# A new order for the opening of a gated-delta attention block: VectorE's first scans, the gates and the first seven keys, and the first unit's work under the substitution

## Chip, core and metric

The kernel runs on one core of one Trainium2 chip. The metric is the device time of one execution in microseconds (us), the median of the runs; less is better. The engines are called PE (TensorE, matmuls and transposes), PEld (its weight loads), DVE (VectorE), ACT (ScalarE), POOL (GpSimd) and SP (SyncE, which issues DMAs). ACT issues DMAs too, and these stand in ACT's own queue.

## What is computed

All inputs are float32. `x` and `fside` are (4, 512, 512), batch by tokens by channels. The reference, cut to what matters:

```python
x = x + attn(wkv(x, fside, fside, w, u, cond), W_qkvz, W_ba, conv_w, dt_bias, A_log, norm_w, W_out)
x = x + ffn(wkv(x, fside, fside, w2, u2, cond), weight, bias)     # signs of weight times its row mean

def wkv(r, k, v, w, u, cond):                 # k = v = fside; decay per channel from w and cond
    ek = exp(min(k, 30)); ekv = ek * v
    nf, df = scan(a = a*decay + ekv_t), scan(b = b*decay + ek_t)         # forward in time
    nb, db = the same scans backward
    euk = exp(min(u + k, 30))
    num = nf + nb - ekv + euk*v;  den = df + db - ek + euk
    return sigmoid(r) * num / max(den, 1e-8) * (0.8 + 0.2*tf)            # tf from cond

def attn(x, ...):                             # 16 query/key heads, 32 value heads of 128
    q, k, v, z = projections of x; a, b = x @ W_ba
    q, k, v = silu(causal convolution of 4 taps along tokens)
    beta = sigmoid(b); g = -exp(A_log) * softplus(a + dt_bias)
    q, k = rmsnorm of both; delta rule in chunks:
        M = strictly lower part of (beta k) k^T * decay(g);  T = (I + M)^-1
        state, out = recurrence over the chunks with T, k, v, q and decay(g)
    return (norm_w * rmsnorm(out) * silu(z)) @ W_out
```

## The kernel before

A **unit** `n` is one batch with one query/key head and its two value heads: 4 x 16 = 64 units. Each unit has six weight slabs of 128 rows: r = 0 query, 1 key, 2 and 3 values, 4 and 5 z. Tokens are taken in four chunks of 128; a chunk's two heads give eight 128x128 matrices M per unit. In batch 0 a slab is loaded (`slab_start`), transposed on PE (`slab_turn`) and copied by ACT (`slab_end`), which also stores it for the later batches.

**The loop** runs over `i`; iteration `i` works on several units at once by a written plan of 22 slots (`plan`, L1044): the recurrence of unit `i-1` (`chunk_w`, `chunk_t`, `chunk_r`), the output of `i-2` and `i-3`, values, query and inverse of unit `i` and the key of unit `i+6`. The order of the plan is the order of every engine's queue. Four units make a group: the 32x32 diagonal blocks of their M go to memory (`key_blocks`), come back with one block to a partition (`group_load`), are inverted by 30 steps of substitution (`group_step`, `group_end`), stored (`blocks_n`, `blocks_t`) and loaded for each unit (`inverse_load`: four `inv_t` and six `inv_n` loads); `inverse_1` to `inverse_4` join them into T. In the loop GpSimd does the substitution; the first group's is done by VectorE.

**The opening** is what has to be there before the loop can run: the first wkv for batch 0 in four channel blocks `cb` (`first_turn` ... `first_end`), written as stages that overlap from block to block; the weights of the gates; the gates (`gates_product` ... `gates_rows`), whose sums go to memory and come back to all partitions (`gap_load`, 512 KB each); keys of units 0 to 5 (projection, taps, Silu, norm by Newton steps, `key_factors`, `key_matrix`); the first group's substitution; and the inverse loads of units 0 and 1. Then the loop begins with `i` = 0, which does unit 0's slabs 2, 3 and 0, values, query and inverse, and unit 6's key. Tiles that later hold other things are lent to the opening (`lent`, `homes`). PSUM has four tags: `pp` 2 banks, `pj` 3, `inv` 1, `st` 2.

A wkv block of the opening, as DVE sees it: limits (`first_limit`), four scans over 512 tokens, `den` from the sum in PSUM, its reciprocal, and the end that writes `cT`. GpSimd makes `ekv` and the terms with `u` (`first_mix`, three products); PE adds the three parts of each sum with the identity (`first_sum`). The order that the stages come in, and where slabs stand among them, is given by this:

```python
for cb in range(KT):
    w = wkv_start(0, 0, cb)
    for i, f in enumerate(stages):
        work.append((i + 4 * cb, cb, f, w))
for i, (_, cb, f, w) in enumerate(sorted(work, key=lambda s: s[:2])):
```

Of the kernel before, what the change touches and what calls it, by code (L numbers as in the profile page):

```python
# [16 lines left out]
P = 128  # L17
# [23 lines left out]
def kernel(  # L41
# [104 lines left out]
    with ExitStack() as main:  # L146
# [24 lines left out]
        for cb in range(KT):  # L171
            at = slice(cb * P, (cb + 1) * P)
            raw = ld.tile([P, NC, P], F32, tag="raw", name=f"raw_k_first_{cb}")
            for t, src in ((raw, fside), (xs[0][:, :, at], x)):
                A.dma_start(out=t, in_=src[0, :, at].rearrange("(c p) d -> p c d", p=P))
            first_raw[cb] = raw

# [4 lines left out]
        for n, v in enumerate((w1, w2, u1, u2)):  # L182
            Q.dma_start(out=wu[:, n, :], in_=v.rearrange("(n p) -> p n", p=P))
        Q.dma_start(out=alog, in_=A_log.partition_broadcast(P))
# [17 lines left out]
        A.activation(nea, alog, AF.Exp)  # L202
        V.tensor_scalar_mul(nea, nea, -1.0)

# [128 lines left out]

        def gates_series(g):

            b, y, e = g["b"], g["y"], g["e"]
            V.tensor_scalar_add(beta[b], beta[b], 1.0)
            V.reciprocal(beta[b], beta[b])
# [21 lines left out]
        def gates_keep(g):  # L360
# [13 lines left out]
                gsum[b][:, 0].rearrange("p c (q r) -> p q c r", r=2),  # L374
            )

        def gates_turn(g):
            g["pt"] = bank("pj", f"ps_gt_{g['b']}")
            T.transpose(g["pt"][: NC * HV, :P], g["flat"][:, : NC * HV], ident)

        def gates_rows(g):
            b, n = g["b"], NC * HV
            rows = wkp.tile([P, S], F32, tag="d", name=f"sp_r_{b}")
            A.copy(rows[:n, :P], g["pt"][:n, :P])
            Q.dma_start(out=gsc[b].rearrange("q (x t) -> (q x) t", t=P), in_=rows[:n, :P])
# [142 lines left out]


# [36 lines left out]
        def key_root(n):  # L566
            root(*units[n]["kroot"])
            key_factors(n)
# [89 lines left out]
        def inverse_load(n):  # L658
# [3 lines left out]
            for d, at in enumerate(blocks):  # L662
# [3 lines left out]
                if d < 3:  # L666
                    for h in range(2):
                        Q.dma_start(
                            out=Tn[blocks[2 * h + (d > 0)], :, at],
                            in_=blocks_n[g, i, d, h * HM : (h + 1) * HM].rearrange("m i j -> i m j"),  # L670
                        )
# [363 lines left out]
        def last_add(b, c):  # L1035
# [80 lines left out]
        INVERSE = (  # L1116
            inverse_1, inverse_1_end, inverse_2, inverse_2_end, inverse_3, inverse_3_end,
            inverse_4, inverse_4_end,
        )

# [27 lines left out]
        for i in range(2):  # L1148
            homes.append(u2p.tile([P, S], F32, tag="q", name=f"lent_q_{i}"))

# [47 lines left out]

        def first_end(w):
            cb, den = w["cb"], w["df"]  # L1200
            e = cT[0][:, cb]
            V.scalar_tensor_tensor(den, w["sum_d"], 1e-8, e, ALU.max, ALU.mult)
            V.reciprocal(den, den)
            V.scalar_tensor_tensor(e, w["sum_n"], scale[:, 0:1], den, ALU.mult, ALU.mult)

        work = []
        stages = (
            first_turn, first_bound, first_limit, first_x, first_mix, (first_scan, "d"), (first_sum, "d"),
            (first_scan, "n"), (first_sum, "n"), first_end,
        )  # L1210
        for cb in range(KT):
            w = wkv_start(0, 0, cb)
            for i, f in enumerate(stages):
                work.append((i + 4 * cb, cb, f, w))
        turned = 0
        for i, (_, cb, f, w) in enumerate(sorted(work, key=lambda s: s[:2])):
            f, *args = f if isinstance(f, tuple) else (f,)
            f(w, *args)
            if i % 6 == 5 and turned < AHEAD:
                if turned == 0:  # L1220
                    for n in range(AHEAD):
                        if n < 2:
                            slab_start(n, 1, homes[n])
                if turned + 2 < AHEAD:
                    slab_start(turned + 2, 1, homes[turned + 2])
                slab_turn(turned, 1)
                slab_end(turned, 1)
                turned += 1
        for n in range(turned, AHEAD):
            slab_turn(n, 1)  # L1230
            slab_end(n, 1)


        wba_raw = ld.tile([2 * HV, D], F32, tag="raw", name="wba_raw")
        Q.dma_start(out=wba_raw, in_=W_ba)
        wbaT = wp.tile([P, KT, 2 * HV], F32, name="wbaT")
        ps = bank("pj", "ps_wba")
        for k in range(KT):
            T.transpose(
                ps[:, k * 2 * HV : (k + 1) * 2 * HV], wba_raw[:, k * P : (k + 1) * P],  # L1240
                ident[: 2 * HV, : 2 * HV],
            )
        A.copy(wbaT.rearrange("p k o -> p (k o)"), ps[:, : KT * 2 * HV])

        cw = wp.tile([P, 4 * HQ, 4], F32, name="cw")
        Q.dma_start(out=cw, in_=conv_w.rearrange("(n p) k -> p n k", p=P))
        g = {"b": 0}

        def first_key(n, tag="pp"):
            project(n, 1, 0, tag)  # L1250
            project(n, 1, 1, tag)

        def first_conv(n):
            tap(n, 1, 0)
            taps(n, 1)

# [213 lines left out]
```

## Time and profile before

| | us |
|---|---|
| median of three runs (lowest, highest) | 3143.19 (3143.12, 3145.72) |
| the profiled execution | 3145.25 |
| its span | 3143.2 |
| PE busy in the span | 2991.7 |
| last `cT` of the first wkv ends | 62.8 |
| DMA issue of the gate sums | 77.3 |
| VectorE's last `key_matrix` of the first group ends | 113.9 |
| first substitution step, end of the transposed copy | 120.6, 143.7 |
| `chunk_w(0,0)`, the start of iteration 1 | 196.3 |
| `chunk_w(1,0)`, the start of iteration 2 | 238.6 |

The times of events are counted from the start of the span. In the lines of a profile, "x" with a number is the count of instructions, and an arrow in brackets names what ended the idle time before an instruction. Most instructions are recorded by one helper, so all have line L80, and tiles tell them apart: `lent_...` are tiles of the first wkv, `dkd` and `dkt` the decay matrices, `L` and `Lt` the blocks of a group, `ps_w` a slab in PSUM or a recurrence product, `wraw` a slab as loaded, `rs_y` and `rs_t` the Newton steps.

### The profile page before, as it was taken

What the parts mean: (1) busy time and instruction counts of PE and PEld (TensorE: products, weight loads), DVE (VectorE), ACT (ScalarE), POOL (GpSimd) and SP (SyncE); (2) the same over time, 40 slices, a digit from 0 to 9 for tenths busy, and PEclk for the clock granted to TensorE, in tenths of its full rate; (3) what the DMA queues carried; (4) which work ended last, traced back from release to release, by engine and by line L of the source; (5) the groups of instructions that cost most, each with busy time, mean ns of one, the idle gap of its engine ahead of it and who ended that gap; (6) DMA issues with size and microseconds to landing.
All of it is one profiled execution on the core that took longest, in us unless ns stands there. A gap on an engine that the chain in (4) does not pass through costs nothing.

```text
span 3143.2 us, 57926 instructions
## 1 busy us (share of the span) xinstructions
PE 2991.7 (95%) x20058; PEld 1979.9 (63%) x20058; DVE 2066.1 (66%) x4738; ACT 1861.3 (59%) x5115; POOL 1313.4 (42%) x3044
## 2 busy tenths in 40 slices
PE   6489999999999999999999999999999999999998
PEld 3256666666666666666666666666666666665664
DVE  7546767667665777668766776667765656577642
ACT  2446666666666666556665666566666666655542
POOL 3216354263522646164432646255442515255302
PEclk9689999999999999999999999999999999999999
DMA  3334544444434323332332422332332322333321
GB/s 75 90 87 140 144 122 127 119 141 132 137 111 142 111 68 92 95 94 85 108 104 89 126 69 88 109 91 84 114 94 74 113 83 84 110 89 96 105 84 54
DMA packets 421875, 320.52 MB, mean 102 GB/s; under 512 B 220176, under 2 KB 329232, under 8 KB 421200
## 3 DMA queue, kind: packets, MB, share of 16 engines
q1 hardware_dynamic: 417360, 314.73, 34.5%
q8 instruction: 160, 2.62, 0.4%
q10 hardware_dynamic: 4224, 2.10, 0.3%
q14 instruction: 131, 1.07, 0.1%
HBM read 246.19 MB, written 70.52 MB: 101 GB/s over the span
## 4 chain that ended last, share of the span: by engine, by line
PE 72%; DVE 17%; ACT 8%; issue 2%; DMA 1%; SPq 0%; POOL 0%; ACTq 0%; DVEq 0%; POOLq 0%
PE ps_p L80 20%; PE ps_out L80 13%; PE ps_z L80 11%; DVE y L80 5%; PE ps_w L80 4%; PE ps_s L80 4%; PE ps_o L80 3%; PE ps_kq L80 2%; PE ps_st L80 2%; DVE f L80 2%; PE ps_f L80 2%; PE ps_j L80 2%; PE ps_i L80 1%; PE ps_v L80 1%; ACT y L80 1%
## 5 line engine op out<-in xcount | busy, mean ns | idle before, releaser
L80 PE MATMUL ps_p<-cT,w 128*128 128x512 f32 x2000 | 956.4, 606 | 13.6 <-ACT w L80 13.6
L80 DVE SCALAR_TENSOR_TENSOR y<-ps_p,cw,y 128x511 f32<-128x511 f32 (+2 forms) x768 | 573.2, 746 | 436.3 <-ACT y L80 421.6
L80 PEld LDWEIGHTS ps_p<-cT,w 128*128 128x128 f32 x2000 | 346.7, 191 | 307.7 <-issue 263.4
L80 PE MATMUL ps_z<-w,cT 128*128 128x256 f32 x2048 | 476.5, 379 | 0.0
L80 PE MATMUL ps_out<-wo,hT 128*128 128x512 f32 x1024 | 465.6, 597 | 7.1 <-DMA wo<-wosc 7.1
L80 PEld LDWEIGHTS ps_z<-w,cT 128*128 128x128 f32 x2048 | 373.7, 190 | 42.5
L80 PEld LDWEIGHTS ps_out<-wo,hT 128*128 128x128 f32 x1024 | 185.5, 191 | 194.8 <-issue 189.4
L80 ACT ACT_TABLE_LOAD x137 | 175.8, 1283 | 160.6 <-DVE y L80 115.9
L80 POOL TENSOR_TENSOR L<-L,t 128x30 f32<-128x30 f32 (+14 forms) x450 | 248.7, 553 | 34.9
L80 ACT ACTIVATE qs<-ps_s,eg 128x128 f32<-128x128 f32 x384 | 120.3, 364 | 239.4 <-PE ps_j L80 136.3
L80 POOL TENSOR_TENSOR t<-L 128x30 f32<-128x30 f32 (+14 forms) x450 | 228.3, 507 | 43.8 <-DMA L<-blocks_m 13.9
L80 POOL TENSOR_SCALAR_AFFINE_SELECT dkd<-dkd 128x1024 f32<-128x1024 f32 x64 | 70.0, 1094 | 396.8 <-DMA dkd<-gsc 272.9
L80 ACT ACTIVATE y<-ps_p,cw 128x512 f32<-128x512 f32 x256 | 173.9, 679 | 70.2 <-PE ps_p L80 69.2
L80 POOL TENSOR_TENSOR rs_t_o<-rs_y_o 128x8 f32<-128x8 f32 x192 | 38.7, 202 | 416.9 <-DVE rs_y_o L80 406.9
L80 ACT ACTIVATE junk<-o 128x128 f32<-128x128 f32 x512 | 157.9, 308 | 75.7 <-DVE o L80 67.6
L80 POOL TENSOR_TENSOR rs_t_k<-rs_y_k 128x4 f32<-128x4 f32 x174 | 55.8, 321 | 348.5 <-DVE rs_y_k L80 339.4
L80 ACT ACTIVATE v<-y 128x512 f32<-128x512 f32 x128 | 80.7, 630 | 203.6 <-DVE y L80 201.0
L80 DVE SCALAR_TENSOR_TENSOR o<-o,rs_y_o,nz 128x128 f32<-128x128 f32 x512 | 189.8, 428 | 1.2 <-POOL rs_y_o L80 1.2
L80 DVE TENSOR_TENSOR x<-x,ps_out 128x512 f32<-128x512 f32 x256 | 168.9, 679 | 25.1 <-PE ps_out L80 24.9
L80 DVE SCALAR_TENSOR_TENSOR r<-ps_s,nbe,vb 128x128 f32<-128x128 f32 x384 | 115.8, 343 | 93.1 <-PE ps_s L80 93.1
L80 ACT COPY w<-ps_w 128x256 f32<-128x256 f32 (+1 forms) x346 | 145.4, 431 | 46.6 <-PE ps_w L80 46.4
L80 ACT ACTIVATE dkt<-dkt,gsum 128x128 f32<-128x128 f32 x512 | 162.6, 392 | 17.4 <-POOL dkt L80 17.3
(270 smaller groups left out, 5565.0 us busy)
## 6 DMA issues: line engine op xcount, KB each, us to landing
w<-wsc SPq DMA_DIRECT2D x288, 256.0 KB, 4.9
dkd<-gsc SPq DMA_DIRECT2D x64, 512.0 KB, 4.3
dkt<-gsc SPq DMA_DIRECT2D x64, 512.0 KB, 4.7
wraw<-in_L_attn_W_qkvz_dram SPq DMA_DIRECT2D x96, 256.0 KB, 3.0
wo<-wosc SPq DMA_DIRECT2D x96, 256.0 KB, 3.7
wsc<-w SPq DMA_DIRECT2D x90, 256.0 KB, 2.1
blocks_m<-dkd SPq DMA_DIRECT2D x256, 32.0 KB, 2.5
L<-blocks_m SPq DMA_DIRECT2D x16, 512.0 KB, 4.9
```

Source lines behind the costliest of these rows:

```text
L80: return lambda *args, **kw: tc.keep_in_program_order(op(*args, **kw))
```

## The change

- Of the eight loads of the first wkv, the two of block 0 stay on ACT's queue; six go to SP, behind three of the small loads. `nea` moves behind the gates' exponentials.
- The first wkv has a written order. `first_end` is split into `first_under`, `first_over` and `first_end`; the limits of the next block stand before the reciprocal, and `first_mix` of the next block is issued beside it. Twelve slabs (keys of units 0 to 6, the gates' weights, unit 0's r = 2, 3, 0) are turned between the sums. Keys of units 0 and 1, and the gates, are summed by channel block as each `cT` comes.
- The logarithm of the gates stands before beta; the cumulative sums are copied from PSUM directly; `gates_turn` uses the gates' bank.
- Keys of the first group: the squares go to GpSimd, the norms to the bank of the gate sums, and Newton steps of two units at a time to VectorE (`root_now`, nine instructions in place of twelve on GpSimd).
- Iteration 0 is gone. Unit 0's work, its z products and the projections of units 4 to 6 stand before the substitution in the queues. `inverse_load` does all `inv_t` loads first; for unit 0 the `inv_n` loads are on ACT's queue. Keys of units 4 to 6 end behind the substitution and in iteration 1 (`job`).

The diff, without names of tiles that only move and without the old order of the opening (shown above). Leading blanks are cut by eight.

```diff
...
-for cb in range(KT):
+def first_load(cb, queue):
     at = slice(cb * P, (cb + 1) * P)
     raw = ld.tile([P, NC, P], F32, tag="raw", name=f"raw_k_first_{cb}")
     for t, src in ((raw, fside), (xs[0][:, :, at], x)):
-        A.dma_start(out=t, in_=src[0, :, at].rearrange("(c p) d -> p c d", p=P))
+        queue.dma_start(out=t, in_=src[0, :, at].rearrange("(c p) d -> p c d", p=P))
     first_raw[cb] = raw
+first_load(0, A)
 tf = const.tile([P, B], F32, name="tf")
 tcond = u2p.tile([P, B, cond.shape[1]], F32, tag="y", name="tcond")
 Q.dma_start(out=tcond, in_=cond.partition_broadcast(P))
-for n, v in enumerate((w1, w2, u1, u2)):
+for n, v in ((0, w1), (1, w2), (2, u1)):
     Q.dma_start(out=wu[:, n, :], in_=v.rearrange("(n p) -> p n", p=P))
+for cb in range(1, KT):
+    first_load(cb, Q)
+Q.dma_start(out=wu[:, 3, :], in_=u2.rearrange("(n p) -> p n", p=P))
 Q.dma_start(out=alog, in_=A_log.partition_broadcast(P))
...
-A.activation(nea, alog, AF.Exp)
-V.tensor_scalar_mul(nea, nea, -1.0)
...
-def gates_series(g):
-    b, y, e = g["b"], g["y"], g["e"]
+def gates_beta(g):
+    b = g["b"]
     V.tensor_scalar_add(beta[b], beta[b], 1.0)
     V.reciprocal(beta[b], beta[b])
+def gates_series(g):
+    gates_beta(g)
+    gates_log(g)
...
-        gsum[b][:, 0].rearrange("p c (q r) -> p q c r", r=2),
+        ps[:, :n].rearrange("p (c q r) -> p q c r", q=HQ, r=2),
...
-    g["pt"] = bank("pj", f"ps_gt_{g['b']}")
-    T.transpose(g["pt"][: NC * HV, :P], g["flat"][:, : NC * HV], ident)
+    bk = g["bank"] if "bank" in g else bank("pj", f"ps_gt_{g['b']}")
+    g["pt"] = bk[:, 2 * NC * HV : 2 * NC * HV + P]
+    T.transpose(g["pt"][: NC * HV], g["flat"][:, : NC * HV], ident)
...
+def root_now(v, y, t):
+    for _ in range(3):
+        V.tensor_tensor(t, y, y, ALU.mult)
+        V.scalar_tensor_tensor(t, t, -0.5, v, ALU.mult, ALU.mult)
+        V.scalar_tensor_tensor(y, t, 1.5, y, ALU.add, ALU.mult)
...
-def inverse_load(n):
+def inverse_load(n, other=Q):
...
-        if d < 3:
-            for h in range(2):
-                Q.dma_start(
-                    out=Tn[blocks[2 * h + (d > 0)], :, at],
-                    in_=blocks_n[g, i, d, h * HM : (h + 1) * HM].rearrange("m i j -> i m j"),
-                )
+    for d, at in enumerate(blocks[:3]):
+        for h in range(2):
+            other.dma_start(
+                out=Tn[blocks[2 * h + (d > 0)], :, at],
+                in_=blocks_n[g, i, d, h * HM : (h + 1) * HM].rearrange("m i j -> i m j"),
...
+def first_under(w):
+    V.scalar_tensor_tensor(
+        w["df"], w["sum_d"], 1e-8, cT[0][:, w["cb"]], ALU.max, ALU.mult
+    )
+def first_over(w):
+    V.reciprocal(w["df"], w["df"])
...
+def first_gates(ks):
+    if ks[0] == 0:
+        g["bank"] = bank("inv", "ps_ba_0")
+    ba = g["bank"][:, : NC * 2 * HV].rearrange("p (c o) -> p c o", c=NC)
+    for k in ks:
+        for c in range(NC):
+            T.matmul(
+                ba[:, c, :], lhsT=cT[0][:, k, c * P : (c + 1) * P], rhs=wbaT[:, k, :],
+                start=(k == c == 0), stop=(k == KT - 1 and c == NC - 1),
+            )
...
+def first_key(n, ks):
+    u = unit(n)[-1]
+    if ks[0] == 0:
+        u["pp1"] = bank("pp" if n < 2 else "pj", f"ps_p_{n}_1")
+    for k in ks:
+        T.matmul(
+            u["pp1"], lhsT=u["w1"][:, k, :], rhs=cT[0][:, k, :], start=(k == 0),
+            stop=(k == KT - 1),
+        )
...
+group0, others = range(GROUP), range(GROUP, AHEAD + 1)
...
+for n in group0:
+    slab(n, 1, homes[n])
+slabs.append((wba_start, wba_turn, wba_end))
+for r in (2, 3, 0):
+    slab(0, r)
+for n in others:
+    slab(n, 1, homes[n] if n < AHEAD else None)
...
+def slabs_on(count):
+    for _ in range(count):
+        if loading:
+            loading.pop(0)[0]()
+        _, turn_it, end_it = slabs.pop(0)
+        turn_it()
+        end_it()
+ws = [wkv_start(0, 0, cb) for cb in range(KT)]
+def first_in(cb):
+    for f in (first_turn, first_bound, first_x):
+        f(ws[cb])
+first_in(0)
+first_in(1)
+first_limit(ws[0])
+first_mix(ws[0])
...
+    w = ws[cb]
+    first_scan(w, "d")
+    if cb == 0:
+        first_in(2)
+    first_sum(w, "d")
+    slabs_on(2 if cb else 0)
+    first_scan(w, "n")
+    if cb == 0:
+        first_in(3)
+    first_sum(w, "n")
+    if cb:
+        for n in range(2):
+            first_key(n, (cb - 1,))
+    if cb > 1:
+        first_gates((0, 1) if cb == 2 else (2,))
+    first_under(w)
+    if cb < KT - 1:
+        first_limit(ws[cb + 1])
+    first_over(w)
+    if cb < KT - 1:
+        first_mix(ws[cb + 1])
+        slabs_on(2 if cb else 1)
+    if cb == 0:
+        Q.dma_start(out=cw, in_=conv_w.rearrange("(n p) k -> p n k", p=P))
+    first_end(w)
...
+first_gates((3,))
+for n in group0:
+    first_key(n, (3,) if n < 2 else (0, 1, 2, 3))
+gates_exp(g)
+A.activation(nea, alog, AF.Exp)
+G.tensor_scalar(nea, nea, -1.0, None, ALU.mult)
+tap(0, 1, 0)
+tap(1, 1, 0)
+gates_log(g)
+gates_sum(g)
+tap(0, 1, 1)
+gates_keep(g)
+gates_turn(g)
+gates_rows(g)
+gap_load(0, "d")
+gap_load(1, "d")
+for r in (4, 5):
+    slab_start(0, r)
+for n in range(2, AHEAD + 1):
+    gap_load(n, "d")
+gap_load(0, "t")
+slab_start(AHEAD + 1, 1)
+tap(0, 1, 2)
+tap(0, 1, 3)
+gates_beta(g)
+first_sums = {}
+def first_silu(n):
+    u = unit(n)[-1]
+    silu(n, 1)
+    sq = u["sq1"] = homes[n]
+    G.tensor_tensor(sq, u["x1"], u["x1"], ALU.mult)
...
+def first_root(ns):
+    at, size = 3 * NC * HV + ns[0] * NC, len(ns) * NC
+    kn = kp.tile([P, size], F32, tag="kn", bufs=2, name=f"kn_first_{ns[0]}")
+    V.tensor_scalar_add(kn, g["ps"][:, at : at + size], HD * EPS)
+    many = root_start(kn, size, f"first_{ns[0]}")
+    root_now(*many)
+    for i, n in enumerate(ns):
+        units[n]["rk"] = many[1][:, i * NC : (i + 1) * NC]
...
+first_silu(0)
+tap(2, 1, 0)
+both(project, 0, 2)
+first_norm(0)
+key_pairs(0, "st")
+taps(1, 1)
+first_silu(1)
+tap(3, 1, 0)
+first_norm(1)
+key_pairs(1, "st")
+taps(2, 1)
+first_silu(2)
+tap(0, 2, 0)
+first_norm(2)
+key_pairs(2, "inv")
+taps(3, 1)
+first_silu(3)
+first_norm(3)
+project(0, 0, 0, "pj")
+project(0, 0, 1, "pj")
+key_pairs(3, "pj")
+both(project, 0, 3)
+first_root((0, 1))
+for n in group0:
+    gap_mask(n, "d")
+for n in (0, 1):
+    key_factors(n)
+for n in group0:
+    both(gap_exp, n, "d")
+for n in (0, 1):
+    first_matrix(n)
+first_root((2, 3))
+for n in (2, 3):
+    key_factors(n)
+gap_mask(0, "t")
+for n in others:
+    gap_mask(n, "d")
+for n in (2, 3):
+    first_matrix(n)
+group_load(0)
+taps(0, 2)
+tap(0, 3, 0)
+silu(0, 2)
+tap(0, 0, 0)
+taps(0, 3)
+taps(0, 0)
+both(gap_exp, 0, "t")
+project(4, 1, 0, "st")
+project(4, 1, 1, "st")
+project(5, 1, 0, "st")
+project(5, 1, 1, "st")
+turn(0, 2)
+turn_end(0, 2)
+silu(0, 3)
+silu(0, 0)
+square(0, 0)
+for r in (4, 5):
+    slab_turn(0, r)
+    slab_end(0, r)
+both(z_product, 0, 0)
+turn(0, 1)
+turn_end(0, 1)
+both(z_product, 0, 1)
+turn(0, 3)
+turn_end(0, 3)
+norms(0, 0)
+norms_copy(0, 0)
+queries(0)
+project(6, 1, 0, "pj")
+project(6, 1, 1, "pj")
+z_silu(0, 0)
+z_silu(0, 1)
+both(gap_exp, 4, "d")
+for j in range(1, BS - 1):
+    group_step(0, j, V)
+group_end(0, V.tensor_copy)
+inverse_load(0, A)
+inverse_load(1)
+gap_load(1, "t")
+both(queries_end, 0)
...
+first_conv(4)
+inverse_1(0)
+inverse_1_end(0)
+inverse_2(0)
+first_conv(5)
+inverse_2_end(0)
+norms(4, 1)
+norms_copy(4, 1)
+inverse_3(0)
+inverse_3_end(0)
+norms_turn(4, 1)
+key_norm(4)
+key_root_now(4)
+inverse_4(0)
+inverse_4_end(0)
+norms(5, 1)
+norms_copy(5, 1)
+gap_load(AHEAD + 1, "d")
+key_pairs(4)
...
+for n, slot in ((5, 6), (6, 12)):
+    job(1, slot, key_pairs, n)
+for n, slot in zip(others, (0, 6, 12)):
+    job(1, slot, key_matrix, n, 0)
+    job(1, slot + 1, key_matrix, n, 1)
+    job(1, slot + 1, key_blocks, n)
+job(1, 0, norms_turn, 5, 1)
+for f in (key_norm, key_root_now):
+    job(1, 0, f, 5)
+for half in range(2):
+    job(1, 2, gap_exp, 5, "d", half)
+    job(1, 8, gap_exp, 6, "d", half)
+job(1, 0, tap, 6, 1, 0)
+job(1, 1, taps, 6, 1)
+job(1, 2, silu, 6, 1)
+job(1, 2, square, 6, 1)
+job(1, 4, norms, 6, 1)
+job(1, 4, norms_copy, 6, 1)
+job(1, 6, norms_turn, 6, 1)
+for f in (key_norm, key_root_now):
+    job(1, 6, f, 6)
+def is_made(i, f, n, *args):
+    z = f in (z_product, z_silu) or f in (slab_start, slab_turn, slab_end) and args[0] > 3
+    return z and n == 0
+for i in range(1, NU - W - 1):
...
-            elif 0 <= i + rest[0] < NU:
-                if i == 0 and (f in INVERSE or f == gap_load and rest[0] > K):
-                    later.append((f, *rest))
-                elif i or f != inverse_load:
-                    f(i + rest[0], *rest[1:])
+            elif 0 <= i + rest[0] < NU and not is_made(i, f, i + rest[0], *rest[1:]):
+                f(i + rest[0], *rest[1:])
```

## The prediction

> **What bounds the kernel now.** I read the page's busy times and slices first, to see whether one engine sets the pace and where it does not.
>
> ```profile
> PE 2991.7 (95%) x20058; PEld 1979.9 (63%) x20058; DVE 2066.1 (66%) x4738; ACT 1861.3 (59%) x5115; POOL 1313.4 (42%) x3044
> ...
> PE   6489999999999999999999999999999999999998
> ...
> PEclk9689999999999999999999999999999999999999
> ```
>
> TensorE is busy 95% overall and 90% or more in every slice but the first three (78.6 us each) and the last. So the loop is paced by TensorE, and only the opening has room. The stage windows (columns: PE, PEld, DVE, ACT, POOL busy, granted clock, DMA share, GB/s) say how much.
>
> ```profile
> 0.00:62.90 62.90, 40.13 (x115) 18.98 (x115) 50.19 (x44) 16.52 (x32) 27.72 (x29) 0.92 0.42 93
> 62.90:120.60 57.70, 40.75 (x162) 26.09 (x162) 29.91 (x76) 27.79 (x61) 14.15 (x36) 0.82 0.32 97
> 120.60:143.70 23.10, 7.92 (x25) 5.07 (x24) 21.00 (x63) 9.36 (x32) 0.00 (x0) 0.57 0.01 4
> 143.70:196.30 52.60, 25.91 (x198) 15.74 (x199) 19.29 (x53) 12.10 (x25) 7.06 (x36) 0.69 0.31 87
> ...
> 196.30:238.60 42.30, 41.05 (x297) 29.16 (x297) 21.88 (x55) 27.56 (x78) 5.48 (x19) 0.92 0.37 106
> ...
> 326.00:370.00 44.00, 43.12 (x312) 28.56 (x311) 32.10 (x70) 29.73 (x80) 16.07 (x36) 1.00 0.41 118
> ```
>
> The first unit's recurrence begins at 196.3 (`chunk_w(0,0)`), the second's at 238.6; after that a unit takes about 44 us, 43.1 of it PE. Up to 196.3 PE works 114.7 us, so 81.6 us lie idle, most of it after 120.6. The chain that ended last and the timeline name the waits there.
>
> ```profile
> 116.97 3.64 DMA L<-blocks_m
> ...
> 143.73 2.87 DMA blocks_t<-Lt
> ...
> 156.20 3.05 DMA wraw<-in_L_attn_W_qkvz_dram
> ```
>
> ```profile
> 120.64 0.20 DVE L80 TENSOR_TENSOR t<-L 128x30 f32<-128x30 f32 x1 [6.79 <-DMA L<-blocks_m]
> ...
> 159.29 1.12 PE L80 MATMUL ps_w<-ident,wraw 128*128 128x128 f32 x4 [26.68 <-DMA wraw<-in_L_attn_W_qkvz_dram]
> ...
> 186.52 0.65 PE L80 MATMUL ps_i<-inv_t,dkd 32*32 32x32 f32 x32 [5.96 <-issue]
> ```
>
> VectorE substitutes alone from 120.64 to 143.71. PE then waits 26.68 us for the next weight slab, whose load stands on SP behind twenty inverse loads, and does unit 0's values and queries only after that. Before 62.9 VectorE is full (50.2 of 62.9), and part of that is contention with GpSimd:
>
> ```profile
> 19.93 4.42 DVE L80 TENSOR_TENSOR_SCAN lent_M<-decay,lent_M 128x512 f32<-128x512 f32 x2
> 24.97 3.35 DVE L80 RECIPROCAL lent_M<-lent_M 128x512 f32<-128x512 f32 x1
> ...
> 54.37 1.20 DVE L80 TENSOR_TENSOR_SCAN lent_f<-decay,lent_vb 128x512 f32<-128x512 f32 x1
> ...
> 238.72 0.95 DVE L80 TENSOR_SCALAR rs_y_o<-rs_t_o 128x8 int32<-128x8 int32 x1
> ```
>
> A scan is 2.2 us beside GpSimd's products and 1.2 with GpSimd idle; the last line, a 0.17 us operation, lies beside a 1.09 us mask.
>
> **The change, stage by stage**, in the clock of the profiled execution.
>
> *A, to the last `cT` (62.83).* Before, ScalarE's first activation waits until 10.5, when its eight load issues are out; with two it can follow the reduction that ends at 5.87. Next bound is `u1`: issued at 2.3, 6.7 us to land, 9.0; its exponential 0.68, two limits 0.7: first scan at 10.5, not 13.9. Chunk 0 still mixes beside its scans: 4 x 1.17 + 3 x 1.1 = 8.0; then 0.7 (denominator), 0.65 (limits of the next chunk), 3.45 (reciprocal), 0.8 (end): 24.1. Chunks 1 and 2 take 4 x 1.17 + 0.7 + 0.65 + 3.45 + 0.8 = 10.3, chunk 3 without limits 9.65, since the three GpSimd products (1.28 each, 3.9 with gaps) fit into reciprocal plus end (4.25). `cT` ends at 54.3: **8.5 gained**. PE's load per chunk (two sums 5.2, slabs 1.8, terms of two keys 1.7, gates up to 2) is 10.7 at most and has about 1.5 us of slack ahead of the denominator. The six moved loads stand on SP before `u2`, `alog` and the slabs: slab 0 lands near 17 instead of 15.3, and is wanted near 20. `cw`, 7.0 us to land, is now ahead of slabs wanted 8 us later.
>
> The Trainium skill (SBUF — State Buffer, section "Who interferes with whom") says that a VectorE instruction with two SBUF inputs blocks against GpSimd reads, and one with a single input outside the 2-port modes does not. The trace shows the scans slowed, and reciprocals unmoved at 3.35 with 0.45 us of a product over them, but none wholly beside GpSimd. By the rule stage A stays as worked out.
>
> *B, to the issue of the gate sums' store (77.29).* Gates of the last term 1.0, then PE must finish two half keys and two whole ones (1.72 + 6.9) before the sums: 54.3 + 0.1 + 1.0 + 8.6 = 64.0. The logarithm ends earlier, at 62.4 (55.4, then 1.2 for the exponentials and two small steps, and 5.8 as from 68.01 to 73.81). Sums 0.9, ScalarE 0.75, VectorE 0.6, wait 0.1, transpose 0.45, copy 0.3: 67.1. 12.8 against 14.5: **1.7 gained**.
>
> *C, to the last `key_matrix` (113.85).* VectorE is free of the gate sums at 66.3: two taps 1.55, beta 1.2, then nine taps of units 1 to 3 (3 x 2.32): 76.0; Silu 0.65, square on GpSimd 1.28, norm on PE 1.0: 79.1. Masks of the four units (4 x 1.2) follow the last square on GpSimd, to 82.8; the first two gap loads land near 73 and 74, 5.9 after the store's issue as before, the next two behind two weight slabs near 78 and 80. Newton of units 0 and 1 is now twelve VectorE operations: 2.4 alone (81.5), or, met by all four masks at 0.9 each, about 85; I take 85. Factors 1.0, matrices 2 x 2.15, second Newton 2.4, factors 0.9, matrices 2 x 2.15: 98.0. That is 30.9 against 36.6: **5.7 gained**. Exponentials (9.4 on ScalarE from 79.4) end at 88.8, ahead of it.
>
> The same section calls the shared port an exclusive lock, which speaks against Newton on VectorE beside masks. If each of nine two-input steps met a 1.09 us mask it would be 9.8; only four masks exist, so the sum by the rule stays near mine.
>
> *D, to the substitution.* Blocks out and back took 6.8; VectorE now does nine taps of unit 0 there, 7.05: **0.3 lost**, start at 105.1.
>
> *E, substitution:* 23.1, unchanged. Under it PE has projections of units 4 to 6 (10.4), z products (6.9), transposes, norms and queries (4): 21 at full clock, with some done before.
>
> *F, to `chunk_w(0,0)` (52.5 before).* From 128.2, store 2.9; four `inv_t` issues 1.9 and landing 2.0: 135.0. The six `inv_n` issues stand on ScalarE (0.5 each) after the landing of `blocks_n`, ahead of unit 4's first tap: 133.8; three taps 2.32: 136.1. `inverse_1` and `inverse_2` run beside it; then Silu, square and tap of unit 5 1.95, its taps 2.32, copies 1.8, product 1.2, copy 0.45, Newton of unit 4 2.4, copy 0.85, pairs 1.0, small waits 0.2: 148.3. 20.1 against 52.5: **32.4 gained**. What was there before goes under E; its price, if that cover fails, is in the rivals.
>
> *G, iteration 1 (42.4 before).* PE loses z and two slab transposes (7.8) and gains pairs of two units and norms (2 to 3). But `slab_end(7,1)` was already what PE waited for (`w` at 203.82), and ScalarE now has in front of it a tap 0.7, eight exponentials 2.45, Silu and square 1.25, two more table loads 2.6: **7.0 later**. Taps of unit 7 then stand behind `key_matrix` and Newton (3.6), and exponentials of unit 6 with a table load (3.7) ahead of slab 3, less overlaps: **6.4**. The last part is shorter without z, but the recurrence's own latency shows: 18 for 22, **4 gained**. Net **9.4 lost**; the bounds are 17 lost (clock falls in the stalls) and 5.2 gained (all fits under PE).
>
> The Trainium skill (TensorE: Matmul & The Clock Gate, Part 1) says that an idle window of about 3.4 us halves the clock and as much work restores it; the 0.57 granted in 120.6 to 143.7 agrees. By it two stalls in G cost some 1.7 each, and the time would be 3108.
>
> Sum: 8.5 + 1.7 + 5.7 - 0.3 + 32.4 - 9.4 = 38.6. The profiled execution took 3145.25 at a span of 3143.2, 2.06 over the median of the runs, 3143.19; from the median: 3104.6. The loop after is unchanged but for the order of inverse loads and a copy that now reads PSUM in the gates; both at nothing, as PE is busy 43.1 of 44 there.
>
> **Rivals.** *Iteration 1 gives nothing back* (G +5.2): 3090.0. For it: PE had 41.05 busy of 42.30; against it: ScalarE's copy was last already.
> *The opening keeps more*: the products contend with the reciprocal after all (nine scan-sized delays of 1.1, 9.9), or PE, at the 0.57 clock of that stage, is some 10 late under the substitution; each 3114.5, both 3124.5.
> *Slower*: `inv_n` now comes after all four `inv_t` on SP, in each of 62 units. If `inverse_2` waited for it, 0.62 us a unit eats the gain; at 1.0 a unit, 62 - 38.6, 3166.6. Against it: the loads leave some 10 us ahead, and the last `inv_n` stays in place.
> *It does not do what it says*: a buffer held longer (gate sums' bank, unit 6's projection) serializes the new order and the opening stays near 196: 3143.
>
> **Chances.** Forecast 0.48, iteration 1 free 0.15, opening keeps more 0.25, smaller gains otherwise 0.04, no change 0.03, slower 0.05. A measurement of this kernel tells about 0.2%, 6.3 us. Faster 0.92, same 0.03, slower 0.05. Range 3092 to 3122: A and C and F at their worse ends one at a time, G at its better end in part.
>
> **What would show it.** Scans near 1.2 after chunk 0 and reciprocals at 3.35; last `cT` near 54; substitution near 105 to 128; no PE wait of tens of us there; `chunk_w(0,0)` near 148; iteration 1 near 52. Wrong if `chunk_w(0,0)` is later than 165, or PE shows new waits past 250.

## The result, and the profile after

The changed kernel takes 3116.55 us (median of four runs, 3115.46 to 3117.31) against 3144.2 for the kernel before on the same chip: a ratio of 0.9911, 95% interval 0.9894 to 0.9929. The forecast was 3104.6 with a range of 3092 to 3122. The direction holds and the time lies in the range, but 27.6 us were gained where 38.6 were forecast. The profiled execution took 3117.31 at a span of 3115.6, against 3143.2 before.

The page of the changed kernel still shows TensorE as the loop's pace, and room only at the two ends (busy share of the span, then tenths in 40 slices):

```profile
PE 2987.3 (96%) x20060; PEld 1978.8 (64%) x20060; DVE 2066.5 (66%) x4788; ACT 1867.3 (60%) x5119; POOL 1306.8 (42%) x3013
...
PE   8679999999999999999999999999999999999998
...
PEclk9789999999999999999999999999999999999999
```

The second and third slices are still low. The stage windows of the changed kernel, cut where its own stages end, say where (columns as before: PE, PEld, DVE, ACT, POOL busy, granted clock, DMA share, GB/s). The rows are the first chunks, the keys, the substitution, the inverse of unit 0, and units 0, 1 and 2 of the loop:

```profile
0.00:53.72 53.72, 42.04 (x152) 22.84 (x153) 43.78 (x43) 18.64 (x35) 23.42 (x29) 0.97 0.61 148
53.72:102.60 48.88, 39.78 (x156) 23.20 (x154) 36.37 (x100) 25.74 (x61) 16.22 (x29) 0.90 0.39 126
102.60:125.70 23.10, 16.44 (x68) 11.77 (x68) 20.96 (x63) 12.29 (x30) 0.00 (x0) 0.77 0.09 26
125.70:147.66 21.96, 7.79 (x138) 6.04 (x138) 10.79 (x31) 5.49 (x9) 2.65 (x6) 0.53 0.43 126
147.66:204.84 57.18, 42.49 (x284) 27.57 (x283) 30.99 (x100) 37.74 (x99) 5.29 (x25) 0.80 0.18 50
204.84:255.18 50.34, 43.40 (x313) 30.67 (x313) 27.18 (x66) 29.85 (x82) 29.50 (x71) 0.89 0.51 149
255.18:303.63 48.45, 47.57 (x337) 32.62 (x336) 37.50 (x77) 34.38 (x88) 29.69 (x59) 1.00 0.48 145
```

The opening ends at 147.66 instead of 196.27: 48.6 us gained, 48.0 forecast. Then iteration 1 takes 57.2 us, of which TensorE works 42.5 at a clock of 0.80; before it took 42.4, with 41.1 busy. Iteration 2 takes 50.3 instead of 45.4. After that the gain is 28.9, and unit after unit begins 28.9 earlier up to unit 23 (what follows is told below). So the opening delivered what was forecast, and 19.7 us were given back in the next two units.

TensorE's own timeline of the changed kernel shows the places (start, length, tiles, and in brackets the wait ahead and its releaser):

```profile
147.66 1.06 PE L80 MATMUL ps_w<-vb,inv_t 128*128 128x128 f32 x4
...
162.77 3.78 PE L80 MATMUL ps_p<-cT,w 128*128 128x512 f32 x4 [3.13 <-ACT w L80]
...
177.67 0.71 PE L80 MATMUL ps_i<-inv_t,dkd 64*64 64x64 f32 x16 [4.18 <-DVE dkd L80]
...
204.84 0.93 PE L80 MATMUL ps_w<-vb,inv_t 128*128 128x128 f32 x4
...
216.49 3.78 PE L80 MATMUL ps_p<-cT,w 128*128 128x512 f32 x4 [6.34 <-ACT w L80]
```

The same rows in the kernel before, up to the start of iteration 3:

```profile
196.27 1.06 PE L80 MATMUL ps_w<-vb,inv_t 128*128 128x128 f32 x4
...
204.43 1.98 PE L80 MATMUL ps_p<-cT,w 128*128 128x512 f32 x4 [0.59 <-ACT w L80]
...
211.56 0.68 PE L80 MATMUL ps_i<-inv_t,dkd 64*64 64x64 f32 x16
...
238.64 0.61 PE L80 MATMUL ps_w<-vb,inv_t 128*128 128x128 f32 x4
...
284.08 0.61 PE L80 MATMUL ps_w<-vb,inv_t 128*128 128x128 f32 x4
```

In the changed kernel `project(7,1)` waits for ScalarE's copy of the slab, `inverse_3(1)` for VectorE's `key_matrix(5)`, `project(8,1)` again for a copy. The second number of a row shows the clock's price: the four matmuls of `project(7,1)` take 3.78 after their wait, and 1.98 at full clock in the kernel before. I cut iteration 1 at `project(7,1)` and `inverse_3(1)` into three stretches and use them below: 15.1, 14.9 and 27.2 us after the change, 8.2, 7.1 and 27.1 before.

ScalarE's timeline of the first stretch shows what stood ahead of the copy:

```profile
149.52 0.71 ACT L80 ACTIVATE y<-ps_p,cw 128x512 f32<-128x512 f32 x1
150.25 1.28 ACT L80 ACT_TABLE_LOAD   x1
151.55 4.78 ACT L80 ACTIVATE dkd<-dkd,gsum 128x128 f32<-128x128 f32 x16
156.35 1.28 ACT L80 ACT_TABLE_LOAD   x1
157.64 0.63 ACT L80 ACTIVATE k<-y 128x512 f32<-128x512 f32 x1
158.30 0.63 ACT L80 ACTIVATE sq<-k 128x512 f32<-128x512 f32 x1
158.95 1.28 ACT L80 ACT_TABLE_LOAD   x1
...
162.15 0.57 ACT L80 COPY w<-ps_w 128x512 f32<-128x512 f32 x1
```

Before, the copy began 7.55 after `chunk_w(0,0)`; now it begins 14.5 after it. The 6.9 between are unit 6's tap, unit 5's eight exponentials (half of the 16), Silu, square, and two of the three table loads. The forecast had 7.0, for the same operations. VectorE's rows ahead of `inverse_3(1)` show why it waits: unit 7's taps, and behind them the second half of `key_matrix(5)`.

```profile
174.28 2.31 DVE L80 SCALAR_TENSOR_TENSOR y<-ps_p,cw,y 128x511 f32<-128x511 f32 x3
176.50 1.12 DVE L80 SCALAR_TENSOR_TENSOR dkd<-ps_kk,nbr,dkd 128x128 f32<-128x128 f32 x4
```

### The profile page after: what moved, and what is told of

The parts are those of the page before. It is cut to its first block, busy times and chain, and to the rows that moved or that the text cites. A ratio compares the mean times of both kernels' runs of the same rounds, so it can differ in the third digit from the quotient of the medians.

```text
span 3115.6 us, 58001 instructions
## 1 busy us (share of the span) xinstructions
PE 2987.3 (96%) x20060; PEld 1978.8 (64%) x20060; DVE 2066.5 (66%) x4788; ACT 1867.3 (60%) x5119; POOL 1306.8 (42%) x3013
## 4 chain that ended last, share of the span: by engine, by line
PE 70%; DVE 15%; ACT 8%; issue 2%; POOL 0%; DMA 0%; DVEq 0%; ACTq 0%; SPq 0%; POOLq 0%
PE ps_p L80 19%; PE ps_out L80 14%; PE ps_z L80 11%; DVE y L80 5%; PE ps_w L80 4%; PE ps_s L80 4%; PE ps_o L80 3%; PE ps_kq L80 2%; PE ps_st L80 2%; DVE f L80 2%; PE ps_f L80 2%; PE ps_j L80 2%; PE ps_i L80 1%; ACT L80 1%; PE ps_v L80 1%
## 5 line engine op out<-in xcount | busy, mean ns | idle before, releaser
L80 ACT ACTIVATE dkt<-dkt,gsum 128x128 f32<-128x128 f32 x512 | 162.5, 392 | 21.8 <-POOL dkt L80 21.6
L80 DVE TENSOR_SCALAR qe<-pss 128x4 f32<-128x4 f32 x64 | 10.3, 162 | 235.6 <-PE pss L80 235.6
```

Of the source, the lines that this page charges most:

```text
L80: return lambda *args, **kw: tc.keep_in_program_order(op(*args, **kw))
```

## The experiments

The theory ahead of the runs: the jobs for keys 4 to 6, which the new order puts into iteration 1, set its length; in iteration 2 it is a mask that came to stand behind other work on GpSimd. The rival: iteration 1 is long because TensorE lost z there, stalls, and falls to half clock. All starts below are from profiles; the times of most of these kernels lie too close together for their intervals to part them.

### What makes iterations 1 and 2 long

**Exponentials of units 5 and 6 early**

```diff
+for n in others:                 # behind slab_end(0, 5), under the substitution
+    both(gap_exp, n, "d")
 both(z_product, 0, 0)
...
-both(gap_exp, 4, "d")            # behind z_silu
...
-for half in range(2):
-    job(1, 2, gap_exp, 5, "d", half)
-    job(1, 8, gap_exp, 6, "d", half)
```

> The gap exponentials of units 5 and 6 leave iteration 1 and stand with unit 4's ahead of z_silu, under the substitution. Theory (ScalarE's and VectorE's jobs for keys 4 to 6 set iteration 1): Silu of unit 4 needs no table load (1.28) any more, chunk_w(0,0) 1.3 earlier, at 146.4; the copy of slab (7,1) comes 2.45 earlier and the two extra table loads with 2.44 of exponentials leave the middle, so iteration 1 falls from 57.2 to 52 to 54, and the time by 4 to 6 us, to about 3111. Rival (iteration 1 is long because TensorE has lost z and its clock falls): iteration 1 stays within 1 us of 57.2, the time near 3115.

Measured: 3110.4 us, ratio 0.9886 (0.9871 to 0.99). `chunk_w(0,0)` at 146.31, as expected; iteration 1 54.2, just outside the expected 52 to 54 and far from the rival. The three stretches are 13.8, 14.0 and 26.5, so 1.3, 1.0 and 0.7 came off. In the first, 2.4 us of exponentials gave only 1.3, since ScalarE now waits 1.03 for VectorE ahead of unit 6's Silu. Exponentials and their table loads are 3 us of iteration 1's excess, no more.

**All jobs of keys 4 to 6 ahead of iteration 1**

```diff
 first_conv(5)
...
+key_norm(5); key_root_now(5); first_conv(6); norms, copy, turn of 6
+key_norm(6); key_root_now(6)
+for n in (5, 6):
+    both(gap_exp, n, "d")
+for n in others:
+    key_pairs(n); first_matrix(n)
...
-every job(1, ...) of units 4 to 6
```

> All jobs of keys 4 to 6 (taps, Silu, norms, Newton, exponentials, pairs, matrices) stand ahead of iteration 1. Theory: chunk_w(0,0) comes 12 to 18 later, at 160 to 166, and iteration 1 falls from 57.2 to 42 to 44: its first stretch (to project(7,1)) from 15.1 to about 8.2, its second (to inverse_3 of unit 1) from 14.9 to about 7.1, the rest stays at 27. Rival (lost z and the clock): iteration 1 stays above 50. The time by itself is no test: about 3115 to 3120 by the theory, 3127 or more by the rival.

Measured: `chunk_w(0,0)` at 164.37, iteration 1 37.3, time 3109.3 (ratio 0.9879, 0.9864 to 0.9894). TensorE's timeline of this kernel has neither of the two waits:

```profile
164.37 1.06 PE L80 MATMUL ps_w<-vb,inv_t 128*128 128x128 f32 x4
...
171.95 1.98 PE L80 MATMUL ps_p<-cT,w 128*128 128x512 f32 x4
...
179.08 0.68 PE L80 MATMUL ps_i<-inv_t,dkd 64*64 64x64 f32 x16
...
201.66 0.61 PE L80 MATMUL ps_w<-vb,inv_t 128*128 128x128 f32 x4
```

and its window of iteration 1 reads

```profile
164.37:201.66 37.29, 33.83 (x258) 22.42 (x257) 21.20 (x57) 24.55 (x74) 4.30 (x17) 0.91 0.30 85
```

The stretches are 7.6, 7.1 and 22.6. This settles the cause: with the jobs gone iteration 1 is 19.9 us shorter, although z is still missing; the rival had 50 or more. Against the changed kernel's window (57.18 long, 42.49 busy) TensorE's idle time falls by 11.2 (14.7 to 3.5) and its busy time by 8.7. About 3 of the 8.7 are the pairs, norms and transposes of keys 5 and 6, reckoned at full clock; the remaining 5.6 or so are the half clock that the waits bring with them. (In iteration 1 TensorE is busy 17.8 us at a clock of 0.50 in the changed kernel, and 6.1 here; half the difference is 5.8.) The theory missed the third stretch: it lost 4.6 too, where I had it unmoved. Of these 4.6, 2.7 are matmuls that run at half clock in the changed kernel, and 1.0 the pairs of unit 6. Paid for by 16.7 us more of serial opening, the whole still gains, as iteration 2 is also 3.2 shorter here: the mask of unit 8 now stands ahead of Newton by itself.

**z back in the loop**

```diff
-    slab_start(0, r); slab_turn(0, r); slab_end(0, r)    # r = 4, 5
-both(z_product, 0, 0); both(z_product, 0, 1); z_silu(0, 0); z_silu(0, 1)
...
 def is_made(i, f, n, *args):
-    return z and n == 0
+    return False
```

> The z products of unit 0, their slabs and Silus are back in iteration 1, as in the kernel before. chunk_w(0,0) stays at 147.7 within 1 by all. The prediction's term (without z the last stretch is 4 us shorter): iteration 1 is 61, the time 3120. Theory (the recurrence's chain sets the last stretch, 27.2 without z against 27.1 with z before): iteration 1 is 57 to 58, the time 3116 to 3117. Rival (z would cover the stalls and hold the clock up): iteration 1 falls below 55.5, the time to 3114 or less.

Measured: `chunk_w(0,0)` at 148.19, iteration 1 60.4, iteration 2 47.8 (its exponentials wait 1.64 for the mask instead of 3.63), time 3116.4 (ratio 0.9905, 0.989 to 0.9919). My theory fell here and the prediction's term came near: taking z out is worth 3.2 us in iteration 1 (4 forecast). Nor does z cover much of the stalls: the jobs of keys 4 to 6 cost iteration 1 18.0 with z (60.4 against the 42.4 of before) and 19.9 without. Together with the run before this changes the reading of the third stretch. It takes 22.6 with neither z nor the jobs, 27.1 with z alone (the kernel before), 27.2 with the jobs alone and 30.2 with both. So its 27.2 equals the 27.1 of before because two things cancel: z taken out (4.5) and the 4.6 that the jobs bring.

**The mask of unit 8 ahead of Newton**

```diff
 job(1, 14, gap_load, AHEAD + 2, "d")     # + both: at slot 14 and 21
 job(1, 21, gap_mask, AHEAD + 2, "d")     # instead of 18 and iteration 2's slot 0
```

> In iteration 1 the gap load of unit 8 is issued ahead of unit 2's inverse loads, and its mask stands ahead of the twelve Newton steps of unit 0's output on GpSimd. Theory (the mask behind Newton made ScalarE's exponentials, the copy of slab (8,1) and project(8,1) late): iteration 2 falls from 50.3 to about 45.4, as in the kernel before, and the time by 4.9, to about 3111.7. Rival (the clock of 0.72 and the loads set iteration 2): it stays at 49 to 50.5 and the time at 3116.

In the kernel before, GpSimd does this mask first and the Newton steps of the output behind it:

```profile
238.54 1.09 POOL L80 TENSOR_SCALAR_AFFINE_SELECT dkd<-dkd 128x1024 f32<-128x1024 f32 x1 [13.83 <-DMA blocks_m<-dkd]
239.75 0.20 POOL L80 TENSOR_TENSOR rs_t_o<-rs_y_o 128x8 f32<-128x8 f32 x1
```

In the changed kernel GpSimd's queue has the twelve Newton steps of unit 0's output first, and ScalarE waits for the mask (last Newton step, the mask, then ScalarE's exponentials and slab copy):

```profile
210.06 0.20 POOL L80 TENSOR_TENSOR rs_y_o<-rs_y_o,rs_t_o 128x8 f32<-128x8 f32 x1
210.37 1.23 POOL L80 TENSOR_SCALAR_AFFINE_SELECT dkd<-dkd 128x1024 f32<-128x1024 f32 x1
...
211.63 2.44 ACT L80 ACTIVATE dkd<-dkd,gsum 128x128 f32<-128x128 f32 x8 [3.63 <-POOL dkd L80]
...
215.88 0.57 ACT L80 COPY w<-ps_w 128x512 f32<-128x512 f32 x1
```

With the edit the mask is done before iteration 2 begins (205.62) and the exponentials start 3.1 after that, not 6.8:

```profile
201.93 1.09 POOL L80 TENSOR_SCALAR_AFFINE_SELECT dkd<-dkd 128x1024 f32<-128x1024 f32 x1 [8.37 <-DMA dkd<-gsc]
...
208.72 2.45 ACT L80 ACTIVATE dkd<-dkd,gsum 128x128 f32<-128x128 f32 x8
212.15 1.28 ACT L80 ACTIVATE dkt<-dkt,gsum 128x128 f32<-128x128 f32 x4 [0.98 <-POOL dkt L80]
```

Iteration 2 is 47.3 instead of 50.3, time 3110.6 (ratio 0.9884, 0.9867 to 0.99). So the mask explains 3.1 of the 4.9. The edit also issues the mask's load earlier, so by itself it does not part the order from the load; but in the changed kernel that load is issued at 201.56 and lands within 4.0 us, ahead of the first Newton step at 206.93, so the 3.63 us wait is the order's. Of the rest about 1.0 lies ahead of `project(8,1)`, where the other mask (`dkt`) still stands behind Newton, and 0.8 in the stretch behind it; that second part I have not taken apart, though the clock of this iteration is 0.92 against 0.96 before.

### What the opening's terms are worth

**GpSimd's products beside the scans.** A first attempt moved only the call of `first_mix`:

```diff
 first_over(w)
-    first_mix(ws[cb + 1])
...
 first_end(w)
+if cb < KT - 1:
+    first_mix(ws[cb + 1])
```

> GpSimd's three products of a chunk stand behind the end of the chunk before, so that they lie beside the scans instead of beside the reciprocal. Theory (scans contend with GpSimd, reciprocals do not): in chunks 1 to 3 some 3.9 us of products lie over 4.8 us of scans, which then last 1.9 to 2.3 each instead of 1.2; 3.0 to 3.9 more a chunk, last cT 9 to 12 later, at 63 to 66, and the time at 3125 to 3128. Rival (the order of the opening and TensorE's sums set stage A, not the contention): scans stay near 1.2 or the last cT moves by less than 4, the time below 3121.

Measured: 3111.1 us, and no scan longer. It was no test: the products wait for the limits alone, and GpSimd has nothing else queued, so they still ran beside the reciprocal (18.34 to 22.24, with the reciprocal from 18.46 to 21.8). The second attempt moved the limits, which the products depend on:

```diff
 first_under(w)
-if cb < KT - 1:
-    first_limit(ws[cb + 1])
 first_over(w)
-    first_mix(ws[cb + 1])
...
 first_end(w)
+if cb < KT - 1:
+    first_limit(ws[cb + 1]); first_mix(ws[cb + 1])
```

> The limits of the next chunk stand behind the end of the chunk before, so that GpSimd's products, which follow the limits, can only lie beside the next chunk's scans. Theory (scans contend with GpSimd, reciprocals do not): in chunks 1 to 3 the first two or three scans last 1.7 to 2.3 instead of 1.2 and the scan of ekv may wait for its product; 3 to 5 more a chunk, last cT at 62 to 68 instead of 53.7, the time at 3124 to 3131. Rival (where the products stand is worth nothing, TensorE's sums and the loads set stage A): last cT within 3 of 53.7, the time below 3120.

Four scans of chunk 1, the reciprocal of that chunk and one product, first in the changed kernel:

```profile
24.01 4.77 DVE L80 TENSOR_TENSOR_SCAN lent_M<-decay,lent_M 128x512 f32<-128x512 f32 x4
29.95 3.34 DVE L80 RECIPROCAL lent_M<-lent_M 128x512 f32<-128x512 f32 x1
...
29.84 1.32 POOL L80 TENSOR_TENSOR lent_at<-lent_at 128x512 f32<-128x512 f32 x1 [6.16 <-DVE lent_at L80]
```

then in this one:

```profile
24.13 7.67 DVE L80 TENSOR_TENSOR_SCAN lent_M<-decay,lent_M 128x512 f32<-128x512 f32 x4
33.20 3.35 DVE L80 RECIPROCAL lent_M<-lent_M 128x512 f32<-128x512 f32 x1
...
25.29 2.17 POOL L80 TENSOR_TENSOR lent_M<-lent_M 128x512 f32<-128x512 f32 x1
```

Beside the scans a product takes 2.17 and the four scans 2.9 more; beside the reciprocal the product takes 1.3 and the reciprocal its 3.35. The last `cT` ends at 64.1 instead of 53.7, `chunk_w(0,0)` comes at 158.13, the time is 3126.7 (ratio 0.9935, 0.9921 to 0.995). The 10.4 us is what this part of the change earns; 8.7 of it are the longer scans of the three chunks. The prediction had 9.9 for it, as the price of its rival.

**Newton on GpSimd again**

```diff
 def first_root(ns):
...
-    root_now(*many)
+    root(*many)
```

> The two paired Newton sequences of the opening run on GpSimd (twelve steps of 0.28) instead of VectorE (nine). Theory: VectorE's steps took 3.2 us each time with one step in a mask; on GpSimd 3.4 us and the masks queue behind or ahead of it, so the last key_matrix ends 1 to 5 later than 95.9, chunk_w(0,0) at 148.5 to 153, the time 3117 to 3121. Rival (the shared port makes VectorE's Newton beside masks costly): the last key_matrix ends earlier, the time falls to 3114 or less.

Measured: the substitution starts at 106.04 instead of 102.68, `chunk_w(0,0)` at 150.99, time 3119.1 (ratio 0.9911, 0.9895 to 0.9928). So Newton on VectorE is worth 3.4 us at the substitution's start; the two masks that slip in ahead of the first `key_matrix` there, 1.09 each, are 2.2 of it.

**Unit 4's taps ahead of the inverse loads**

```diff
 group_end(0, V.tensor_copy)
+first_conv(4)
 inverse_load(0, A)
...
-first_conv(4)
```

> Unit 4's taps, Silu and square stand ahead of the inverse loads on ScalarE and VectorE. Theory (after the substitution the serial order tap, six issues, taps, taps is the path): taps of unit 4 run at 126 to 128 instead of 131.2 to 133.5, taps of unit 5 end near 135.5 instead of 139.1, and chunk_w(0,0) comes 3 to 4 earlier, at 144; iterations 1 and 2 keep their 57.2 and 50.3, the time is 3113. Rival (the six issues come 2 us later on ScalarE and the inverse then waits for inv_n): chunk_w(0,0) within 1 of 147.7, the time 3116.

Measured: `chunk_w(0,0)` at 145.50, 2.2 earlier, iteration 1 56.9, time 3113.6 (ratio 0.9895, 0.9879 to 0.9912). Between the two: the taps come earlier, but ScalarE now waits 2.4 for them ahead of a table load and Silu, with the six issues behind.

### A version that beats both

Two kernels put the findings together: exponentials 4 to 6 and first taps 4 to 6 under the substitution, the other taps and Silus while the inverse loads land, one Newton for three keys, matrices of 4 to 6 behind the recurrence's copies in iteration 1, the mask of unit 8 early.

```diff
+tap(4, 1, 0); tap(5, 1, 0); tap(6, 1, 0, (wkp, "k"))      # ahead of the substitution's steps
 inverse_load(0, A); inverse_load(1)
+taps(4, 1); both(queries_end, 0); taps(5, 1); Silu and square of 4 and 5
 inverse_1(0); inverse_1_end(0)
+tap(6, 1, 1); tap(6, 1, 2)
 inverse_2(0); inverse_2_end(0)
+tap(6, 1, 3); Silu and square of 6
 inverse_3(0); inverse_3_end(0)
+norms of 4 and 5, one column a product
 inverse_4(0); inverse_4_end(0)
+norms of 6; key_pairs(4, "pj"); job(1, 0, others_root)    # one Newton for 4 to 6
+matrices of 4, 5, 6 at slots 3, 6, 12 of iteration 1
```

> Exponentials of units 4 to 6 ahead of z_silu; first taps of units 4 to 6 under the substitution, their other taps and Silus while the inverse loads land and between the inverse's steps; one Newton for the three; matrices of units 4 to 6 in iteration 1 behind the recurrence's copies; mask of unit 8 ahead of Newton. Theory: chunk_w(0,0) at 140 to 142, iteration 1 at 39 to 42, iteration 2 at 46 to 47.3, so iteration 3 starts 24 to 30 earlier than the changed kernel's 255.2, and the time is 3087 to 3092. Rival (VectorE's matrices still hold the inverse's bank in iteration 1): iteration 1 at 48 or more, the time 3098 or more.

Measured: 3097.6 us (ratio 0.9844, 0.9829 to 0.9858); `chunk_w(0,0)` only at 147.63, iteration 1 43.7, iteration 2 47.6. Most of the miss is my own: twelve one-column products for the norms (24 instructions, 5.4 us of TensorE at half clock) stood ahead of `chunk_w(0,0)`. But the substitution also started at 104.52, 1.8 later than in the changed kernel. The second kernel moved the products behind `chunk_w(0,0)`:

```diff
+job(1, 0, others_norms); job(1, 1, others_copy)      # four 32-wide products a unit
+job(1, 2, others_turn);  job(1, 5, others_root)      # one Newton for units 4 to 6
+for n, slot in zip(others, (6, 12, 14)):
+    job(1, slot, key_pairs, n)                       # and both halves of key_matrix
```

> As e7_all_moves, but the norms, Newton and pairs of units 4 to 6 stand behind chunk_w(0,0), in iteration 1, and the norms are four 32-wide products a unit again instead of four one-column products. Theory: the 5.4 us of one-column products at the half clock and unit 4's pairs (1.9) leave TensorE's way to chunk_w(0,0), which comes at 141 to 143.5 instead of 147.6; iteration 1 grows by at most 2, to 43 to 46; the time falls by 3 to 5 from 3097.6, to about 3093. Rival (VectorE's Newton and matrices then hold iteration 1's recurrence): iteration 1 at 48 or more, no gain over e7_all_moves.

Measured: 3092.1 us (3090.8 to 3094.9), ratio 0.983 (0.9815 to 0.9845), below the changed kernel's interval. Its windows of iterations 1 and 2:

```profile
138.34:184.05 45.71, 38.99 (x307) 26.42 (x308) 27.75 (x86) 26.30 (x76) 8.31 (x31) 0.91 0.27 72
184.05:233.30 49.25, 44.49 (x313) 31.59 (x313) 24.47 (x65) 29.95 (x82) 28.75 (x71) 0.87 0.54 155
```

Unit 2 begins at 233.3 instead of 255.2. `chunk_w(0,0)` came 2.7 us ahead of the expected range and 9.3 ahead of the first of the two kernels. Of these 9.3, 3.3 are no merit of the move: the substitution started at 101.20 here, with the same code up to there (1.5 of the 3.3 is the clock in chunk 0, last section). The intervals of the two kernels overlap, so only that both beat the changed kernel is shown; iteration 2 still waits 4.26 us for the copy of slab (8,1), so some of this is left.

## Why the prediction was right, and where it was not

The stages, each as gain forecast and gain measured, from the same marks:

| stage | forecast | measured | marks after |
|---|---|---|---|
| A, last `cT` | 8.5 | 9.1 | 53.72 |
| B, store of the gate sums issued | 1.7 | 1.2 | 66.95 |
| C, last `key_matrix` | 5.7 | 7.6 | 95.88 |
| D, substitution starts | -0.3 | 0.0 | 102.68 |
| E, substitution | 0 | 0 | 125.76 |
| F, `chunk_w(0,0)` | 32.4 | 30.7 | 147.66 |
| G, iteration 1 | -9.4 | -14.8 | 204.84 |
| iteration 2 | 0 | -4.9 | 255.18 |
| the rest | 0 | -1.3 | end |

- **A to F held**: 48.0 forecast, 48.6 measured, no single stage off by more than 1.9. That is about the scatter of one profile: in seven kernels with the same code ahead of it (the changed kernel and six of the experiments) the substitution starts between 101.2 and 104.5. C was better because Newton of units 0 and 1 ended at 82.5, not 85: only one of its steps met a mask (0.98 instead of 0.17), since two masks had run before the last squares. F gained 1.7 less. There was no new wait of tens of us under the substitution.
- **The contention rule held.** The Trainium skill (SBUF — State Buffer, "Who interferes with whom") says that a VectorE instruction with at most one SBUF input, outside the 2-port modes, does not contend with GpSimd, and the trace of before had no reciprocal wholly beside a product. The rows above now show both sides, 3.34 beside products and scans at 2.2.
- **G is the step that failed**: 9.4 lost forecast, 14.8 measured. "7.0 later" measured 6.9. "6.4" measured 7.8, and that it came near is luck, for the parts are others: 4.2 is the wait for `key_matrix(5)`, 2.5 the half clock (1.8 in `project(7,1)` alone), 1.0 the pairs of unit 5. The exponentials of unit 6, which the sum put into this term, began only at 179.90, behind the wait, and TensorE waited no more than 0.50 for the copy behind them. "The last part is shorter without z, 4 gained" measured nothing: z is worth 4.5 there by itself, but key 6's work also reaches into that stretch, where the sum had counted all of it as ahead, and brings 4.6 with its clock.
- **The half clock was at nothing in G's sum.** It takes 2.5 in the second stretch and 2.7 in the third, 5.2 of the 5.4 by which G was off. The prediction named it beside the sum, with 3.4 by the page on the clock gate read as two stalls of 1.7, and in the bound of 17 lost.
- **Iteration 2 was outside the sum.** The prediction called the loop after iteration 1 unchanged and priced no order on GpSimd there. The code lists Newton ahead of the mask in both kernels, but on GpSimd the mask ran first before and Newton first after. So the order of the plan is not always the order of an engine's queue, as the description of the loop has it. What made the two change places is not shown. Nothing in the diff says so; a comparison of GpSimd's queue in the two programs does. The range had no share for these 4.9 us; that the time still lies in it is luck in this part.
- **The rivals.** By the total alone 3116.6 lies nearer to "the opening keeps more" (3114.5) than to the forecast. The marks decide against it: the opening gave the gain forecast, and the loss lies behind it. The slower rival (`inv_n` behind `inv_t` in each unit) found no place: every steady iteration has the length it had before, and the gain stays at 28.9 from iteration 3 to iteration 24.
- **The last 1.3**: 1.5 of it goes at one place, in iteration 24, and is the clock and not a wait (last section); around iterations 58 to 60 and at the end another 1.0 comes and 0.8 goes, which I have not followed.

## What to carry to other kernels

When work is taken out of a serial opening and put "under" the first loop iterations, price the iteration that receives it as a new schedule: list for each engine what now stands ahead of the operation that the pacing engine waits for, and add the clock that the waits cost. Here three keys' jobs cost 19.9 us in iteration 1 against 16.7 when done in plain sequence ahead of it; only spread over waits that already existed were they cheap. And an experiment that moves a call must move what the call depends on: on a queue with nothing else in it, the later line runs at the same moment.

## What the runs showed of the hardware that was not expected

The same wait does not cost the same in every execution. In iteration 24, 19 us after its start, TensorE waits 2.50 us for `r`, before and after. First the row, and two windows of 2 us around and behind it, of the kernel before; then of the changed kernel:

```profile
1282.56 0.75 PE L80 MATMUL ps_w<-r,inv_t 128*128 128x128 f32 x4 [2.50 <-DVE r L80]
...
1281.92:1283.92 2.00, 1.36 (x6) 0.97 (x7) 1.97 (x6) 1.06 (x4) 0.00 (x0) 1.00 0.00 0
1283.92:1285.92 2.00, 2.00 (x13) 1.39 (x12) 1.95 (x9) 2.00 (x8) 0.00 (x0) 1.00 0.00 0
```

```profile
1253.62 1.22 PE L80 MATMUL ps_w<-r,inv_t 128*128 128x128 f32 x4 [2.50 <-DVE r L80]
...
1253.00:1255.00 2.00, 1.38 (x5) 1.35 (x6) 1.97 (x6) 1.08 (x4) 0.00 (x0) 0.60 0.00 0
1255.00:1257.00 2.00, 2.00 (x3) 0.67 (x2) 1.95 (x9) 1.48 (x6) 0.00 (x0) 0.55 0.00 0
```

In one execution the clock stays at 1.00, in the other it averages 0.60 and 0.55 over these 4 us, and 1.5 us of the gain is gone from there on. Of the twelve kernels' profiles, six show the lower clock at this place and six do not. The Trainium skill (TensorE: Matmul & The Clock Gate, Part 1) puts a free-running window of 3.4 us behind the clock's changes, by which it would be a matter of phase, which no run here tests; the page speaks of an idle window of about 3.4 us, and a wait of 2.50 was enough here. The same toss stands in chunk 0: the first six sums take 4.54 at a clock of 0.5 to 0.72 in the changed kernel, and 2.84 at 1.00 in `e5_mix_by_scans` and `e9_norms_later`, whose last `cT` comes 1.3 to 1.4 sooner for it. Over the profiles of the twelve kernels, the time from the start of unit 2's recurrence to the end lies between 2855.8 and 2860.4. A difference of 4 us in one profiled span is therefore no evidence here. The marks inside a profile are better evidence, within their own scatter of some 1.7 us either way at the substitution.
